# Cross-attention on one core: score tiles from one product over four heads and two products of 154 columns, with second copies of the high queries made by GpSimd

## The chip, the core and the metric

The kernel runs on one core of a Trainium2 chip. A core has five engines with a queue each, which run in order and wait for each other through semaphores: TensorE (PE in the profile; its weight loads are listed apart as PEld), VectorE (DVE), ScalarE (ACT), GpSimd (POOL) and SyncE (SP), which here issues nearly all DMAs. The metric is the device time of one execution in microseconds. A trace of one execution gives the start and the duration of every instruction.

## The reference, cut to what matters

There are 32 sequences of 512 query rows with 640 channels, and 77 key rows of 1024 channels for each sequence. Twenty heads of 32 channels attend; the result goes through an output matrix, and a bias and the input are added. The slices for the object, other and ip branches are empty, since the context has only the 77 text rows, and add nothing.

```python
residual = hidden_states
ehs_txt = encoder_hidden_states[:, :77]
q = _heads(hidden_states @ to_q_w)
s = jnp.einsum('bhqd,bhkd->bhqk', q, _heads(ehs_txt @ to_k_w)) / sqrt(32)
p = jax.nn.softmax(s, axis=-1)
out = _merge(jnp.einsum('bhqk,bhkd->bhqd', p, _heads(ehs_txt @ to_v_w)))
out = out @ to_out_w + to_out_b + residual
```

All of it is in float32. TensorE gets its operands in the type fp32r, which holds fewer bits. The kernel therefore splits a matrix into a high part (a cast on ScalarE) and a low part (the source less the high part, on VectorE or GpSimd) and adds three products: high by high, high by low, low by high. These are the three entries of `PAIRS` (L127).

## The kernel before

**Prologue (to about 274 us).** The context is transposed and split, keys and values of all sequences are computed with the 640 channels on partitions, and both are written to DRAM as high and low parts (`split_keys`, L207, tile `k_dram`, L97; `split_values`, L221). `split_keys` has its high cast, its low subtract and one DMA for each group of 512 key rows and each chunk of channels; groups but the last go through the GpSimd queue, the last through SP.

**Slots.** The channels make 5 chunks of 128, which is four heads each. A slot (`slot(n)`, L660) is one chunk j of one sequence b, n = 5b + j, 160 slots in all. One slot works on many things at once, because stages of earlier chunks are dealt out over later slots:

- `queries(n+1)` (L428): 15 products of 512 columns give the next chunk's queries, transposed (channels on partitions), in one PSUM bank `pq`. `split_q(n+1)` (L442) casts them on ScalarE to `qt[:, 0]` and subtracts on VectorE to `qt[:, 1]`.
- `scores(n, t)` for t = 0 to 3 (L447): for 128 queries the scores against all four heads at once. The keys `kb` are block diagonal (head i has its 32 partitions and its 77 columns, the rest is zero), so 128 channels by 308 columns give 4 heads of 77 scores. Three products of 308 columns make one tile `sc` (3 buffers). Then VectorE takes the negated maximum `nm` of each head (L461).
- `exps(n, t)` (L466): four exponentials on ScalarE for each tile, with row sums.
- `sums` and `normalize(n-1)` (L479, L484): the reciprocals on VectorE and one multiply on GpSimd over the whole chunk of the slot before.
- `transpose_p(n-1)` (L490): a 32 by 32 block transpose on VectorE into the single buffer `z`, then four DMAs to a DRAM tile `pd`. One slot later `load_p` (L506) reads it back as `raw`, with keys on partitions, and again one slot later `cast_p`, `rest_p` and `last_p` (L513 to L533) split it: two casts on ScalarE, one subtract on VectorE and one subtract of 64 partitions on GpSimd.
- `values` (L539): 6 products of 512 columns into `pa`; `sum_a`, `high_a`, `low_a` (L553 to L572) fold and split the result to `at`.
- `piece` (L603): parts of the output projection of the sequence before, 24 products of 320 columns in a slot, into two banks `po`. `finish` (L611) adds residual and bias from `xr` on VectorE, which frees the bank, and stores. `load_residual` (L574) loads `xr`, `add_bias` (L580) adds the bias to it on GpSimd.
- For the next sequences: `load_x`, `transpose_x`, `split_x` (L244 to L264); `refill` (L647) loads the next keys and values.

**What sets the order.** The program is scheduled by hand: the queue of each engine follows the order of the calls in `slot`. In a steady slot GpSimd has `last_p`, `normalize`, then `add_bias` (L706, in all slots but j = 1), then the low parts of `split_x` (two in slot j = 2, three in slot j = 3). VectorE has, in the middle of the slot, the transpose to `z`, the subtract of `split_q`, the maximum of score tile 3, `finish`. ScalarE goes from the exponentials of score tile 3 to `cast_p`, `high_a` and `rest_p` of the next slot. SP issues `load_keys` in slots j = 0 and j = 2 (four DMAs each, two before `load_p` and two behind), `load_values` in slots 1 and 3, `load_x` in slot 4, and `load_residual` in slots 1 to 4. The bias of a residual tile is added one slot after the load: tile 3, loaded in slot 4, in slot 0.

Of the kernel before, what the change touches and what calls it, by code (L numbers as in the profile page):

```python
# [8 lines left out]
F32 = mybir.dt.float32  # L9
FPR = mybir.dt.float32r  # L10
AF = mybir.ActivationFunctionType
ALU = mybir.AluOpType
# [39 lines left out]
def kernel(  # L52
# [49 lines left out]
    def split(hi, lo, src):  # L102
        nc.scalar.copy(hi, src)  # L103
        nc.vector.tensor_tensor(lo, src, hi.bitcast(F32), ALU.subtract)
# [102 lines left out]
    def split_keys(g, j):  # L207
        g0, gn = GROUPS_KV[g]
        ks = kvt.tile([P, 2, G], FPR, tag="ks", name="ks")
        split(ks[:, 0, :gn], ks[:, 1, :gn], pks.pop(j)[:, :gn])  # L210
        engine = nc.gpsimd if g + 1 < len(GROUPS_KV) else nc.sync
        engine.dma_start(
            k_dram[:, j, :, g0 : g0 + gn].bitcast(F32), ks[:, :, :gn].bitcast(F32)
        )

    def values_of(g, j, pool):

# [175 lines left out]
    nc.sync.dma_start(bias, bo.unsqueeze(0).to_broadcast([P, C]))  # L393
    kbs, vbs, pnb = [], [], []
    for g, (j0, nj) in enumerate(GROUPS):
        kb = main.tile([P, nj, 2, KCOLS], FPR, name=f"kb{g}")
        nc.gpsimd.memset(kb.bitcast(F32), 0.0)
        kbs.append(kb)
    for n in range(2):
        pn = main.tile([P, NQ * HPC, KPAD], F32, name=f"pn{n}")  # L400
        nc.gpsimd.memset(pn, 0.0)
        pnb.append(pn)
    qts = [main.tile([P, 2, S], FPR, name=f"qt{n}") for n in range(2)]
    z = main.tile([P, NBLK, NQ, Q], F32, name="z")
    for g, (j0, nj) in enumerate(GROUPS):
        vb = main.tile([P, nj, 2, 2, P], FPR, name=f"vb{g}")
# [2 lines left out]

    def load_keys(b, g, heads=range(HPC)):  # L410
        j0, nj = GROUPS[g]
        src = k_dram[:, j0 : j0 + nj, :, b * NKEY : (b + 1) * NKEY].bitcast(F32)
        for i in heads:
            r = slice(i * HD, (i + 1) * HD)
            nc.sync.dma_start(kbs[g][r, :, :, i * NKEY : (i + 1) * NKEY].bitcast(F32), src[r])

    def load_values(b, g, segments=SEGMENTS):
        j0, nj = GROUPS[g]
# [23 lines left out]
    def split_q(n):  # L442

        qt, pq = qts[n % 2], pqs.pop(n)
        split(qt[:, 0, :], qt[:, 1, :], pq)

    def scores(n, t):  # L447
        b, j = divmod(n, NC_)
        g = GROUP_OF[j]
        qt, kb = qts[n % 2], kbs[g]  # L450
        sc = ps.tile([P, S], F32, tag="sc", name="sc", bufs=3)
        for m, (a, c) in enumerate(PAIRS):
            nc.tensor.matmul(  # L453
                sc[:, :KCOLS],
                qt[:, a, t * P : (t + 1) * P],
                kb[:, j - GROUPS[g][0], c],
                start=(m == 0),
                stop=(m == 2),
            )
        nm = main.tile([P, HPC], F32, tag="nm", name="nm", bufs=3)  # L460
        nc.vector.tensor_reduce(  # L461
            nm, sc[:, :KCOLS].rearrange("p (h k) -> p h k", k=NKEY), AX.X, ALU.max, negate=True
        )
        return sc, nm
# [95 lines left out]
    def high_a(n):  # L560
        if n >= N - NC_ + 1:
            at = xpool[0].tile([P, 2, S], FPR, tag="xt", name="at", bufs=7)
        else:
            at = late[0].tile([P, 2, S], FPR, tag="at", name="at", bufs=8)
        nc.scalar.copy(at[:, 0, :], pas[n][:, 0])
        ats[n] = at
# [93 lines left out]
    def slot(n, beside=()):  # L660
        b, j = divmod(n, NC_)
        ahead, more = n + 1 < N, b + 1 < B
        back, first = PIECES[j]
        bo_, has_out = b - back, b >= back
        xsplits = SPLIT_X.get(j, ((), ())) if more and n > LATE else ((), ())
        turns = TRANSPOSE_X.get(j, ((), (), ())) if more and b else ((), (), ())
        if b == 1 and j < 2:
            turns = (((), (), ()), ((0, 1), (2,), ()))[j]
        taken = takes.get(n)

        filling = taken is not None and not has_out
        if not filling:
            refill(b, j, 0)
        if taken is not None:
            cast_p(taken)
        if n - 1 in takes:
            high_a(takes[n - 1])
        s = scores(n, 0)
        if taken is not None:
            rest_p(taken)  # L680
        rs = sums(n - 1) if n else None
        if taken is not None:
            last_p(taken)
        if n:
            normalize(n - 1, rs)
        if n - 1 in takes:
            low_a(takes[n - 1])
        exps(n, 0, *s)
        if ahead:
            queries(n + 1, 0, 2)  # L690
        s = scores(n, 1)
        if n - LAG + 1 in pds and n > LATE:
            load_p(n - LAG + 1)
        if filling:
            refill(b, j, 0)
        if n == NC_:
            load_x(b + 1, (2, 3))
        for k in WO.get(n, ()):
            nc.sync.dma_start(wos[0][:, k].bitcast(F32), wo_dram[:, k].bitcast(F32))
        refill(b, j, 1)  # L700
        finish()
        if j == 4 and b and b + 2 < B:
            load_x(b + 2, (0, 1))
        if j in RESIDUAL and b >= RESIDUAL[j][0]:
            load_residual(b - RESIDUAL[j][0], RESIDUAL[j][1])
        if j in BIAS and b >= BIAS[j][0]:  # L706
            add_bias(b - BIAS[j][0], BIAS[j][1])
        exps(n, 1, *s)
        for i in turns[0]:
            transpose_x(b + 1, i)  # L710
        if ahead:
            queries(n + 1, 2, NC_)
        s = scores(n, 2)
        if not ahead:
            exps(n, 2, *s)
            piece(bo_, first)
            s = scores(n, 3)
        if j == 3 and has_out:
            piece(bo_, first)
            finish()  # L720
        if n and has_out:
            transpose_p(n - 1)
        if ahead:
            split_q(n + 1)
            exps(n, 2, *s)
        if n and not has_out:
            transpose_p(n - 1)
        if j == 4 and b + 2 < B:
            load_x(b + 2, (0, 1) if not b else (2, 3))
        for c in xsplits[0]:  # L730
            split_x(b + 1, c)
        if not ahead:
            exps(n, 3, *s)
            finish()
            piece(bo_, first + 1)
            take(taken)
            return
        if has_out:
            if j != 3:
                piece(bo_, first)  # L740
        else:
            s = scores(n, 3)
        if taken is not None:
# [158 lines left out]
```

## Time and profile before

| | |
|---|---|
| median of 3 runs | 1960.85 us (1959.88 to 1962.95) |
| profiled execution, its own time | 1961.89 us |
| its span | 1959.8 us |
| granted TensorE clock over the span | 0.992 |
| busy share of PE, PEld, ACT, DVE, POOL | 97%, 87%, 78%, 73%, 51% |
| DMA packets | 568279 (431.28 MB, mean 220 GB/s) |
| score products (L453) | 1920 of 308 columns, 379.1 us busy |
| exponentials (L471) | 2560 of 128x77 |
| normalize (L486) | 160, mean 2278 ns |
| transpose to z (L493) | 160, mean 1512 ns |
| subtract of split_q (L104) | 160 of 128x512, mean 654 ns |
| add_bias (L581) | 128 of 128x640, mean 1576 ns |

The busy share of PE counts overlapping matmuls with modelled ends, so that it says little about how much time a shorter matmul would save. The chain of waits names the work that ended last at each moment; it says more about what sets the end. Times inside a slot are read from the timelines of the engines.

### The profile page before, as it was taken

What the parts mean: (1) busy time and instruction counts of PE and PEld (TensorE: products, weight loads), DVE (VectorE), ACT (ScalarE), POOL (GpSimd) and SP (SyncE); (2) the same over time, 40 slices, a digit from 0 to 9 for tenths busy, and PEclk for the clock granted to TensorE, in tenths of its full rate; (3) what the DMA queues carried; (4) which work ended last, traced back from release to release, by engine and by line L of the source; (5) the groups of instructions that cost most, each with busy time, mean ns of one, the idle gap of its engine ahead of it and who ended that gap; (6) DMA issues with size and microseconds to landing.
All of it is one profiled execution on the core that took longest, in us unless ns stands there. A gap on an engine that the chain in (4) does not pass through costs nothing.

```text
span 1959.8 us, 36241 instructions
## 1 busy us (share of the span) xinstructions
PE 1909.2 (97%) x10332; PEld 1704.8 (87%) x10332; DVE 1436.2 (73%) x2334; ACT 1534.3 (78%) x6210; POOL 1002.3 (51%) x648
## 2 busy tenths in 40 slices
PE   9999997899999999999999999999999999999997
PEld 7787896798988989989999988889989998988896
DVE  4444345778788888888888777787878878878774
ACT  3232237888889888888888888899888988888982
POOL 1000033655566555555556555666556665566643
PEclk9999998999999999999999999999999999999999
DMA  9878869888888888888998888888898888888874
GB/s 187 185 182 234 197 159 238 219 226 226 226 229 234 223 234 232 231 228 222 235 236 230 230 212 238 229 235 223 226 235 231 226 228 226 226 226 228 226 212 135
DMA packets 568279, 431.28 MB, mean 220 GB/s; under 512 B 195344, under 2 KB 477072, under 8 KB 568080
## 3 DMA queue, kind: packets, MB, share of 16 engines
q1 hardware_dynamic: 564848, 417.65, 83.0%
q0 software_dynamic: 3136, 11.14, 1.6%
q8 instruction: 84, 1.38, 0.3%
q14 instruction: 115, 0.94, 0.2%
q10 hardware_dynamic: 96, 0.16, 0.0%
HBM read 247.17 MB, written 181.64 MB: 219 GB/s over the span
## 4 chain that ended last, share of the span: by engine, by line
PE 21%; DMA 19%; issue 17%; ACT 16%; DVE 12%; POOL 11%; SPq 3%; DVEq 0%; POOLq 0%; ACTq 0%
DMA raw<-pd 8%; ACT pn L471 8%; DMA pd<-z 8%; POOL pn L486 7%; PE pq L434 6%; PE po L588 6%; POOL pp L531 3%; DVE pp L524 3%; PE pv L191 3%; PE sc L453 2%; PE pk L191 2%; ACT xt L262 2%; ACT aw L556 2%; DVE nm L461 2%; DVE z L493 2%
## 5 line engine op out<-in xcount | busy, mean ns | idle before, releaser
L471 ACT ACTIVATE pn<-sc,nm 128x77 f32<-128x77 f32 x2560 | 802.6, 335 | 76.6 <-DVE nm L461 74.3
L588 PE MATMUL po<-wo_s,at 128*128 128x320 f32 x3840 | 626.0, 311 | 21.5 <-DVE xr L617 14.2
L434 PE MATMUL pq<-xt,wq_s 128*128 128x512 f32 x2400 | 605.7, 393 | 0.0
L588 PEld LDWEIGHTS po<-wo_s,at 128*128 128x128 f32 x3840 | 576.6, 189 | 32.2 <-DVE xr L617 24.6
L531 POOL TENSOR_TENSOR pp<-raw,pp 64x512 fp32r<-64x512 f32 x160 | 211.1, 1319 | 663.6 <-ACT pp L523 390.4
L471 ACT ACTIVATION_READ_ACCUMULATOR pn<-sc,nm 128x1 f32 x2560 | 545.2, 213 | 0.0
L434 PEld LDWEIGHTS pq<-xt,wq_s 128*128 128x128 f32 x2400 | 437.0, 188 | 75.2
L453 PE MATMUL sc<-kb,qt 128*128 128x308 f32 x1920 | 379.1, 306 | 13.9 <-ACT pn L471 10.4
L486 POOL TENSOR_TENSOR pn<-pn,rs 128x1232 f32<-128x1232 f32 x160 | 364.4, 2278 | 32.9 <-DVE rs L481 20.5
L453 PEld LDWEIGHTS sc<-kb,qt 128*128 128x128 f32 x1920 | 325.5, 189 | 59.3 <-ACT pn L471 12.3
L493 DVE STREAM_TRANSPOSE z<-pn 128x1280 f32<-128x1280 f32 x160 | 241.8, 1512 | 176.1 <-POOL pn L486 166.7
L461 DVE TENSOR_REDUCE nm<-sc 128x4 f32<-128x308 f32 x640 | 294.5, 462 | 41.3 <-PE sc L453 39.2
L524 DVE TENSOR_TENSOR pp<-raw,pp 128x1024 fp32r<-128x1024 f32 x160 | 195.5, 1222 | 91.8 <-ACT pp L517 86.7
L545 PE MATMUL pa<-pp,vb 128*128 128x512 f32 x960 | 253.3, 399 | 1.6 <-DVE pp L524 0.8
L558 DVE TENSOR_TENSOR pa<-pa,aw 64x512 f32<-64x512 f32 x320 | 222.7, 696 | 31.5 <-ACT aw L556 22.2
L263 POOL TENSOR_TENSOR xt<-xs,xt 128x512 fp32r<-128x512 f32 x160 | 204.4, 1296 | 37.8 <-ACT xt L262 36.9
L556 ACT COPY aw<-pa 64x1024 f32<-64x1024 f32 x160 | 162.0, 1013 | 69.5 <-PE pa L545 66.7
L545 PEld LDWEIGHTS pa<-pp,vb 128*128 128x128 f32 x960 | 175.3, 189 | 32.2 <-DVE pp L524 1.1
L517 ACT CAST pp<-raw 128x1024 fp32r<-128x1024 f32 x160 | 168.8, 1055 | 43.2 <-DMA raw<-pd 43.0
L581 POOL TENSOR_TENSOR xr<-xr,bias 128x640 f32<-128x640 f32 x128 | 201.6, 1576 | 0.1
L191 PE MATMUL pk<-ct,wk_s 128*128 128x512 f32 (+1 forms) x600 | 140.5, 394 | 8.2 <-ACT ct L103 6.3
L191 PEld LDWEIGHTS pk<-ct,wk_s 128*128 128x128 f32 x600 | 116.2, 195 | 30.8 <-ACT ct L103 7.2
(42 smaller groups left out, 1347.0 us busy)
## 6 DMA issues: line engine op xcount, KB each, us to landing
pd<-z SPq DMA_DIRECT2D x640, 160.0 KB, 3.9
raw<-pd SPq DMA_DIRECT2D x160, 512.0 KB, 4.0
xs<-in_x_dram SPq DMA_DIRECT2D x128, 320.0 KB, 6.2
xr<-in_x_dram SPq DMA_DIRECT2D x128, 320.0 KB, 4.1
out_dram<-xr SPq DMA_DIRECT2D x127, 320.0 KB, 4.1
raw<-pd SPq DMA_DIRECT2D x160, 128.0 KB, 4.2
v_dram<-vs SPq DMA_DIRECT2D x80, 192.0 KB, 3.9
k_dram<-ks POOLq DMA_DIRECT2D x20, 512.0 KB, 3.4
```

The source lines that it names most:

```text
L191: nc.tensor.matmul(held[j][:, :gn], w[:, k, a, :], cts[g, k][:, c, :gn], start=(k == 0 and n == 0), stop=(k == NK - 1 and n == 2),)
L434: nc.tensor.matmul(pqs[n], wq_s[:, k, a, j * P : (j + 1) * P], xts[b, k][:, c, :], start=(k == 0 and m == 0), stop=(k == NC_ - 1 and m == 2),)
L453: nc.tensor.matmul(sc[:, :KCOLS], qt[:, a, t * P : (t + 1) * P], kb[:, j - GROUPS[g][0], c], start=(m == 0), stop=(m == 2),)
L461: nc.vector.tensor_reduce(nm, sc[:, :KCOLS].rearrange("p (h k) -> p h k", k=NKEY), AX.X, ALU.max, negate=True)
L471: nc.scalar.activation(pnb[n % 2][:, at, :NKEY], sc[:, i * NKEY : (i + 1) * NKEY], AF.Exp, bias=nm[:, i : i + 1], accum_out=sms[n][:, at : ...
L486: nc.gpsimd.tensor_tensor(pf, pf, rs.unsqueeze(2).to_broadcast([P, NQ * HPC, NKEY]), ALU.mult)
L493: nc.vector.transpose(z.rearrange("p b t j -> p t b j"), pn.rearrange("p (t h) k -> p t (h k)", t=NQ).rearrange("p t (b i) -> p t b i", i=Q),)
L524: nc.vector.tensor_tensor(pp[:, 2:4, :], raw[:, 0:2, :], pp[:, 0:2, :].bitcast(F32), ALU.subtract)
L531: nc.gpsimd.tensor_tensor(pp[64:, 4, :], raw[:64, 2, :], pp[:64, 4, :].bitcast(F32), ALU.subtract)
L545: nc.tensor.matmul(pas[n][:, p, :], vb[:, p, t, :], pp[:, c, :], start=(c == p), stop=(t == 1),)
L558: nc.vector.tensor_tensor(pa[64 * p : 64 * p + 64, 0], pa[:64, p], aw[:, p], ALU.add)
L588: nc.tensor.matmul(pos[b, t, h][:, :HALF], ats[b * NC_ + j][:, a, t * P : (t + 1) * P], wos[0][:, j, c, h * HALF : (h + 1) * HALF], start= ...
```

## The change

The high queries by the low keys, and the low queries by the high keys, were two products of 308 columns, each over all four heads. Now one product has 154 columns and serves two heads: its stationary operand `qt[:, 1]` has the low queries of heads 0 and 1 in partitions 0 to 63 and a copy of their high queries in partitions 64 to 127; the keys `kc[..., 0]` have the high keys of heads 0 and 1 in partitions 0 to 63 and their low keys in 64 to 127. The sum over 128 partitions is both cross products at once. `qt[:, 2]` and `kc[..., 1]` do the same for heads 2 and 3. The product of high by high stays as it was, with keys `kb`.

`split_q` now has one cast on ScalarE, two copies of 64x512 on GpSimd that move the high queries to the other half of the partitions, and two subtracts of 64x512 on VectorE in place of one of 128x512. `load_keys` issues two DMAs for each head, one for `kb` and one for `kc`. `split_keys` writes `k_dram` with three DMAs in place of one, in another order of the parts. `add_bias` moves: in slots 0, 2 and 3 it stands ahead of `scores(n, 0)`, and with that ahead of `last_p` and `normalize` in GpSimd's queue; in slot 4 it stands behind the copies.

```diff
-        engine.dma_start(
-            k_dram[:, j, :, g0 : g0 + gn].bitcast(F32), ks[:, :, :gn].bitcast(F32)
-        )
+        dst = k_dram.rearrange("(h r) c w n -> r c w h n", h=2)[:, j, :, :, g0 : g0 + gn]
+        engine.dma_start(dst[:, 0].bitcast(F32), ks[:64, :, :gn].bitcast(F32))
+        for half in range(2):
+            engine.dma_start(dst[:, 1, half].bitcast(F32), ks[64:, 1 - half, :gn].bitcast(F32))
...
-        kb = main.tile([P, nj, 2, KCOLS], FPR, name=f"kb{g}")
+        kb = main.tile([P, nj, KCOLS], FPR, name=f"kb{g}")
+        kc = main.tile([P, nj, 2, KCOLS // 2], FPR, name=f"kc{g}")
...
-    qts = [main.tile([P, 2, S], FPR, name=f"qt{n}") for n in range(2)]
+    qts = [main.tile([P, 3, S], FPR, name=f"qt{n}") for n in range(2)]
...
-            r = slice(i * HD, (i + 1) * HD)
-            nc.sync.dma_start(kbs[g][r, :, :, i * NKEY : (i + 1) * NKEY].bitcast(F32), src[r])
+            r, half = slice(i * HD, (i + 1) * HD), i % 2 * NKEY
+            nc.sync.dma_start(
+                kb[r, :, i * NKEY : (i + 1) * NKEY].bitcast(F32), src[r, :, i // 2, :]
+            )
+            nc.sync.dma_start(kc[r, :, :, half : half + NKEY].bitcast(F32), src[r])
...
-        split(qt[:, 0, :], qt[:, 1, :], pq)
+        nc.scalar.copy(qt[:, 0, :], pq)
+        lower, upper = slice(0, 64), slice(64, P)
+        halves = ((lower, upper), (upper, lower))
+        for w, (r, other) in enumerate(halves):
+            nc.gpsimd.tensor_copy(qt[other, 1 + w, :], qt[r, 0, :].bitcast(F32))
+        for w, (r, other) in enumerate(halves):
+            nc.vector.tensor_tensor(
+                qt[r, 1 + w, :], pq[r], qt[r, 0, :].bitcast(F32), ALU.subtract
+            )
...
-        for m, (a, c) in enumerate(PAIRS):
+        half = KCOLS // 2
+        for m, (cols, keys_) in enumerate(
+            (
+                (slice(0, KCOLS), kb[:, jg]),
+                (slice(0, half), kc[:, jg, 0]),
+                (slice(half, KCOLS), kc[:, jg, 1]),
+            )
+        ):
             nc.tensor.matmul(
-                sc[:, :KCOLS],
-                qt[:, a, t * P : (t + 1) * P],
-                kb[:, j - GROUPS[g][0], c],
+                sc[:, cols],
+                qt[:, m, t * P : (t + 1) * P],
+                keys_,
...
+        bias_now = j in BIAS and b >= BIAS[j][0]
+        if bias_now and (j != 4 or not ahead):
+            add_bias(b - BIAS[j][0], BIAS[j][1])
         s = scores(n, 0)
...
-        if j in BIAS and b >= BIAS[j][0]:
-            add_bias(b - BIAS[j][0], BIAS[j][1])
         exps(n, 1, *s)
...
             split_q(n + 1)
+            if bias_now and j == 4:
+                add_bias(b - BIAS[j][0], BIAS[j][1])
             exps(n, 2, *s)
```

More of the change, by code (lines that the diff above doesn't have):

```diff
@@ L395 @@
     for g, (j0, nj) in enumerate(GROUPS):
-        kb = main.tile([P, nj, 2, KCOLS], FPR, name=f"kb{g}")
-        nc.gpsimd.memset(kb.bitcast(F32), 0.0)
-        kbs.append(kb)
+        kb = main.tile([P, nj, KCOLS], FPR, name=f"kb{g}")
+        kc = main.tile([P, nj, 2, KCOLS // 2], FPR, name=f"kc{g}")
+        for tile_ in (kb, kc):
+            nc.gpsimd.memset(tile_.bitcast(F32), 0.0)
+        kbs.append((kb, kc))
     for n in range(2):
@@ L411, in load_keys @@
         j0, nj = GROUPS[g]
+        kb, kc = kbs[g]
         src = k_dram[:, j0 : j0 + nj, :, b * NKEY : (b + 1) * NKEY].bitcast(F32)
         for i in heads:
-            r = slice(i * HD, (i + 1) * HD)
-            nc.sync.dma_start(kbs[g][r, :, :, i * NKEY : (i + 1) * NKEY].bitcast(F32), src[r])
+            r, half = slice(i * HD, (i + 1) * HD), i % 2 * NKEY
[3 more added lines that the diff above has]
+            nc.sync.dma_start(kc[r, :, :, half : half + NKEY].bitcast(F32), src[r])
     def load_values(b, g, segments=SEGMENTS):
@@ L449, in scores @@
         g = GROUP_OF[j]
-        qt, kb = qts[n % 2], kbs[g]
+        qt, (kb, kc) = qts[n % 2], kbs[g]
+        jg = j - GROUPS[g][0]
         sc = ps.tile([P, S], F32, tag="sc", name="sc", bufs=3)
-        for m, (a, c) in enumerate(PAIRS):
+        half = KCOLS // 2
[6 more added lines that the diff above has]
+        ):
             nc.tensor.matmul(
-                sc[:, :KCOLS],
-                qt[:, a, t * P : (t + 1) * P],
-                kb[:, j - GROUPS[g][0], c],
+                sc[:, cols],
+                qt[:, m, t * P : (t + 1) * P],
+                keys_,
                 start=(m == 0),
```

## The prediction

> **What bounds the kernel now.** I read the busy shares first:
>
> ```profile
> PE 1909.2 (97%) x10332; PEld 1704.8 (87%) x10332; DVE 1436.2 (73%) x2334; ACT 1534.3 (78%) x6210; POOL 1002.3 (51%) x648
> ```
>
> TensorE looks like the bound, and the change takes work from it. The chain of waits, asked for 980 to 1060 us (a steady stretch of eight slots), says otherwise:
>
> ```profile
> 1036.03 1.11 ACT pn L471 x7
> 1037.14 2.06 issue x2
> 1039.20 1.30 POOL pp L531
> 1040.50 0.07 issue
> 1040.57 2.29 POOL pn L486
> 1042.85 0.02 issue
> 1042.88 1.52 DVE z L493
> ...
> 1045.82 5.34 DMA pd<-z
> ...
> 1051.23 6.22 DMA raw<-pd
> ```
>
> Columns: start, length, what held the end. No PE line stands in those 80 us. The chain runs from the exponentials of score tile 3 through ScalarE's casts ("issue x2" covers cast_p, high_a and rest_p), last_p and normalize on GpSimd to the transpose on VectorE. VectorE's timeline shows how it gets back to the exponentials:
>
> ```profile
> 1001.77 1.51 DVE L493 STREAM_TRANSPOSE z<-pn 128x1280 f32<-128x1280 f32 x1 [1.18 <-POOL pn L486]
> 1003.21 0.65 DVE L104 TENSOR_TENSOR qt<-pq,qt 128x512 fp32r<-128x512 f32 x1
> 1003.78 0.46 DVE L461 TENSOR_REDUCE nm<-sc 128x4 f32<-128x308 f32 x1
> ```
>
> The reader is to see that the subtract of split_q lies between the transpose and the maximum of tile 3, which the exponentials of tile 3 wait for (ScalarE: from 1004.37). That closes a loop of one slot. Slot 4 to slot 0, 992.15 to 1001.74 us: transpose 1.55, subtract 0.58 (start to start), maximum 0.46, exponentials 1.23, casts 2.08, last_p 1.41, normalize 2.36 with the small gaps, 9.6 us and no idle link. Over 28 sequences normalize ends follow each other by means of 9.58 (slot 4 to 0), 11.11 (0 to 1), 10.16 (1 to 2), 9.88 (2 to 3) and 10.32 us (3 to 4): 51.05 a sequence. What exceeds 9.58: in 0 to 1, cast_p waits 1.28 us (plus an overlap of 0.12) for raw; in 1 to 2, high_a waits some 0.4 behind VectorE; in 2 to 3 the exponentials come 0.34, in 3 to 4 0.77 us after the maximum, since ScalarE has split_x casts.
>
> ```profile
> DVE z L493 <- POOL pn L486: 166.7, 148, 2.6
> ACT pp L517 <- DMA raw<-pd: 43.0, 31, 3.7
> ```
>
> In this list of waits (total, times, longest) the transpose waits for normalize in 148 of 160 slots, and cast_p for a DMA once per sequence. TensorE's timeline, at the end of slot 0:
>
> ```profile
> 1003.50 1.03 PE L588 MATMUL po<-wo_s,at 128*128 128x320 f32 x6
> 1004.70 1.15 PE L588 MATMUL po<-wo_s,at 128*128 128x320 f32 x6 [0.16 <-DVE xr L617]
> 1005.69 0.59 PE L453 MATMUL sc<-kb,qt 128*128 128x308 f32 x3
> ```
>
> Once a sequence it waits for VectorE and loses 0.66 us on the mean; slots 1 to 4 take 10.08 to 10.11. TensorE alone needs about 50.4 us a sequence, just under the loop's 51.05. Both run nearly full, and the loop is the longer.
>
> **The change part by part.** *Score products.* Starts follow each other by 0.142 us at 308 columns, 0.147 at 320 and 0.230 at 512: a line of 0.43 ns a column plus 9 ns. After the wait above, six products of 320 take 0.99 us (1004.70 to 1005.69) where six take 0.875: a weight load that nothing hides costs 0.115. A product of 154 columns streams in 0.066 us and can't hide that. So it costs 0.076 (the line) to 0.124 (the load and 9 ns); I take 0.124, since the load has a row of its own and the line is only drawn out to 154. A tile goes from 0.426 to 0.390: 20 tiles save 0.7 us a sequence (2.6 at the other end). It is off the loop: nothing gained at the end.
>
> The Trainium skill (TensorE: Matmul & The Clock Gate, section LDWEIGHTS) speaks against halving the columns: a weight load takes its columns over 1.2 GHz whatever the rows, so 107 ns for 128, more than the 66 ns of the stream; the 0.115 agrees. With 107 ns and 9 a tile would save 0.052, 1.0 us a sequence, and with the same page's gap of an isolated matmul, 67 ns, 3.0; the end would be the same by either.
>
> *Two subtracts for one, on the loop.* Rows by form:
>
> ```profile
> L558 DVE TENSOR_TENSOR pa<-pa,aw 64x512 f32<-64x512 f32 x320 | 222.7, 696 | 31.5 <-ACT aw L556 22.2
> L104 DVE TENSOR_TENSOR qt<-pq,qt 128x512 fp32r<-128x512 f32 x160 | 104.7, 654 | 7.8 <-ACT qt L103 7.8
> ```
>
> 64 partitions are no cheaper than 128. The second subtract adds 0.58 us between transpose and maximum in every slot. In 1 to 2 it counts fully, +0.58; in 2 to 3 ScalarE's 0.34 hides part, +0.24; in 3 to 4 the 0.77 hides it. If ScalarE were free there, +0.9 more. Behind the longer VectorE queue wait the maximum, the residual add and TensorE's bank.
>
> *Copies.* No row has a GpSimd copy. Below: memset of 1232 and 1848 elements takes 1127 and 1643 ns, a line that gives 0.53 us at 512. Above: the two-input 64x512 of last_p, 1.32. I take 0.75, since a copy has one input like the memset but reads too. They start when normalize ends, beside the transpose and the subtracts, and end before those or with them; TensorE reads them over 2 us later. At 1.32 each, split_x and bias behind them make last_p 0.35 us late in slot 3, +0.35 a sequence.
>
> The Trainium skill (GPSIMD Engine Reference, section 3.1) measured 769 ns for 512 elements; no run here shows it, and the sum doesn't need it.
>
> *add_bias ahead of last_p.* In slots 2 and 3 GpSimd is idle there (last_p waited 4 to 6 us and 1.4 to 2 us) and xr landed about 2.5 us before last_p. In slot 4 it stands behind the copies, off the loop. Slot 0 is the trouble: SP issues that load late in slot 4, among input loads and stores of z.
>
> ```profile
> 991.27 0.49 SPq L577 DMA_DIRECT2D xr<-in_x_dram  x1
> 996.23 1.60 SPq L251 DMA_DIRECT2D xs<-in_x_dram  x2
> 998.77 0.94 SPq L415 DMA_DIRECT2D kb<-k_dram  x2
> 1000.29 0.38 SPq L509 DMA_DIRECT2D raw<-pd  x1
> ```
>
> Its landings, taken one by one, come 3.9 to 8.4 us after the issue, median 6.8, which is 0.24 us after last_p starts. The loop gives it 0.58 more; bias takes 1.58: last_p and normalize stand 1.3 us behind it (0 if it lands 1.3 us sooner, 2.9 with the latest).
>
> *Key loads.* Slots 0 and 2 get four more DMAs, each about 0.47 us of SP; no more than two stand ahead of raw. In slot 0 the raw load already waits for pd; two more issues cost 0 to 0.94, 58 KB more in front of it 0.25 at 228 GB/s. I take +0.6 of 0 to 1.2. In slot 2 cast_p has over 2 us to spare. If that cover were gone, a second +0.6.
>
> *Slots 4 to 0 to 1 together*, from the transpose of slot 4 to cast_p of slot 1. The engines' side: 2 x 0.58 + 1.3 = 2.46 more, less the 1.40 it waited, +1.06. The DMA side: +0.6. The later one counts, one by one over 27 sequences +1.2 on the mean.
>
> *Prologue.* GpSimd issues 3 DMAs for 1, 20 times, at up to 0.73 us each (the k_dram row): 29 us, beside 239 us of idle GpSimd before 274 us. ScalarE waits 36 us for those landings already, TensorE hardly: +2 us with the first ten slots, 0 to 10.
>
> **Sum:** 0.58 + 0.24 + 1.2 = 2.0 us for each of 29 full sequences, 58; with 2 for the start, +60. Of the profiled execution's 1961.9 that makes 2022; it stands 1 us above the median, so **2021 us**.
>
> **The rivals.** *TensorE sets the pace after all* (not slower). The profile says that it infers releasers; TensorE has no idle in slots 1 to 4, and ScalarE's aw waits for it in slots 0, 1 and 4 (0.7, 0.4, 0.3 us on the mean). If the loop only follows TensorE and has at least 2.0 us of room a sequence that the chain doesn't show, the 0.7 to 2.6 saved on TensorE count: 29 times that is 20 to 75, 1886 to 1941 us, and 1941 by the price taken. Against it: after each aw the exponentials wait once more for the maximum, and the chain has no PE line. Chance 0.12.
>
> *The bias add in slot 0 doesn't wait.* If SP's later queue leaves xr landing 1.3 us earlier, the pair costs the DMA side's 0.6: 1.42 x 29 = 41, 2003 us. For it, landings scatter by 4.5 us; against it, SP's order ahead of that load is unchanged. Chance 0.20.
>
> *Short products are slow.* No row is below 308 columns. If 154 take as long as 512, 0.230, TensorE needs 50.4 + 20 x (0.142 + 0.460 - 0.426) = 53.9 a sequence: +2.9 x 29 = 83, 2045 us, and more beyond. It decides from 0.21 us per product on. Against it, all four sizes lie on one line. Chance 0.10.
>
> **How the numbers follow.** The forecast has 0.55 (its own range 2003 to 2045), the other 0.03 is no change. Low end of the slower cases: no bias wait, no DMA cost, 0.82 x 29 = 24, 1985 us. High end: bias wait 1.55 and DMA 1.2 (pair +1.6), slow copies 0.35, 2.8 x 29 = 80 and 10 for the prologue, 2050. I widen to 1978 to 2056, which leaves out the first rival and half of the third. A change under 0.2% can't be told from none. Slower: 0.55 + 0.20 + 0.10 = 0.85; same 0.03; faster 0.12.
>
> **What would show it.** Right: the chain still without PE; two subtracts of about 0.65 us between transpose and maximum; normalize from slot 4 to 0 over 10.1 us; bias of slot 0 waiting for xr, last_p starting as it ends; new TensorE waits for VectorE or GpSimd in each slot; 154-column starts 0.08 to 0.12 apart. Wrong: subtracts well under 0.58, a loop that has room, or PE lines in the chain.

## The result, and the profile after

The changed kernel takes 2112.44 us (median of 4 runs, 2107.1 to 2117.95); the kernel before took 1961.53 us (1959.88 to 1962.95) in the same comparison. The ratio is 1.077 (95% interval 1.0748 to 1.0792): 151 us slower, 2.5 times the 60 us that the prediction gave. The profiled execution took 2117.95 us, its span is 2116.1 us, and the granted TensorE clock over the span is 0.956 (0.992 before).

The busy line of the page of the changed kernel, and its groups by form (line, engine, operation, tiles, count; busy us, mean ns of one; idle time ahead and what ended it):

```profile
PE 1947.5 (92%) x10332; PEld 1724.5 (81%) x10332; DVE 1583.5 (75%) x2494; ACT 1540.0 (73%) x6210; POOL 1253.5 (59%) x1010
```

```profile
L611 PE MATMUL po<-wo_s,at 128*128 128x320 f32 x3840 | 654.5, 319 | 113.9 <-DVE xr L640 107.7 <-DVE at L593 4.4 <-ACT at L588 1.8
...
L458 DVE TENSOR_TENSOR qt<-pq,qt 64x512 fp32r<-64x512 f32 x320 | 214.5, 670 | 9.8 <-ACT qt L452 5.3
L604 POOL TENSOR_TENSOR xr<-xr,bias 128x640 f32<-128x640 f32 x128 | 207.3, 1621 | 121.7 <-DMA xr<-in_x_dram 95.6 <-PE sc L476 13.1 <-issue 5.2
...
L456 POOL CAST qt<-qt 64x512 fp32r<-64x512 f32 x320 | 195.3, 610 | 40.8 <-ACT qt L452 22.9
```

The subtracts and the copies last what the rows of before let one expect (670 and 610 ns). What grew is a wait in the first line: TensorE waits 107.7 us for VectorE's `finish` (`xr`) to free a `po` bank. The same row before, with 14.2 us:

```profile
L588 PE MATMUL po<-wo_s,at 128*128 128x320 f32 x3840 | 626.0, 311 | 21.5 <-DVE xr L617 14.2 <-DVE at L570 4.4 <-ACT at L565 1.5
```

The place is the end of slot 0, once a sequence. TensorE's timeline there (start, length, instruction, in brackets the idle time ahead and what ended it):

```profile
1017.49 1.08 PE L611 MATMUL po<-wo_s,at 128*128 128x320 f32 x6
1022.66 1.97 PE L611 MATMUL po<-wo_s,at 128*128 128x320 f32 x6 [4.08 <-DVE xr L640]
1024.42 0.46 PE L476 MATMUL sc<-kb,qt 128*128 128x308 f32 x1
1024.68 0.54 PE L476 MATMUL sc<-kc,qt 128*128 128x154 f32 x2
1025.02 2.85 PE L441 MATMUL pq<-xt,wq_s 128*128 128x512 f32 x6
```

Before, the same place showed an idle time of 0.16 us (at most 1.06 us in any steady slot). Now TensorE stands for 4.08 us, and the products that follow are slow: six of 512 columns take 2.85 us (1.58 in slot 0). The stretches of one sequence, a slot each from j = 0 to 4, show why (start and end, length, busy time of the engines, granted clock, DMA share, GB/s):

```profile
1008.89:1024.42 15.53, 11.05 (x59) 9.76 (x58) 11.54 (x19) 10.82 (x46) 8.05 (x6) 0.92 1.03 242
1024.42:1036.33 11.91, 11.91 (x59) 10.63 (x58) 9.06 (x15) 7.43 (x34) 7.04 (x5) 0.81 0.68 180
1036.33:1046.16 9.83, 9.83 (x59) 8.91 (x58) 8.76 (x15) 8.86 (x35) 6.45 (x6) 1.00 0.75 193
1046.16:1055.98 9.82, 9.82 (x59) 8.91 (x58) 8.06 (x14) 9.46 (x39) 8.53 (x7) 1.00 0.88 213
1055.98:1066.02 10.04, 10.03 (x59) 8.96 (x58) 7.73 (x14) 9.20 (x39) 8.18 (x8) 1.00 0.84 207
```

After the stand the granted clock is below 1 in slots 0 and 1. Over the steady slots 10 to 154 the clock is at half speed for 126.3 us, in 29 stretches of one or two pieces of 3.41 us, one stretch a sequence; before it never was. Slots 2 to 4 take 9.8 to 10.0 us, less than the 10.1 of before: the shorter products are in there.

What makes VectorE late is seen on GpSimd and VectorE in the same slot 0:

```profile
1012.52 2.51 POOL L604 TENSOR_TENSOR xr<-xr,bias 128x640 f32<-128x640 f32 x1 [2.87 <-DMA xr<-in_x_dram]
1015.11 1.30 POOL L554 TENSOR_TENSOR pp<-raw,pp 64x512 fp32r<-64x512 f32 x1
1016.48 2.27 POOL L509 TENSOR_TENSOR pn<-pn,rs 128x1232 f32<-128x1232 f32 x1
```

```profile
1012.37 1.23 DVE L547 TENSOR_TENSOR pp<-raw,pp 128x1024 fp32r<-128x1024 f32 x1
...
1018.79 1.51 DVE L516 STREAM_TRANSPOSE z<-pn 128x1280 f32<-128x1280 f32 x1 [3.72 <-POOL pn L509]
1020.22 1.35 DVE L458 TENSOR_TENSOR qt<-pq,qt 64x512 fp32r<-64x512 f32 x2
1021.60 0.48 DVE L484 TENSOR_REDUCE nm<-sc 128x4 f32<-128x308 f32 x1
1022.11 0.49 DVE L640 TENSOR_TENSOR xr<-po,xr 128x320 f32<-128x320 f32 x1
```

The bias addition waits for its load, `last_p` and `normalize` stand behind it, the transpose waits 3.72 us, the two subtracts follow it, and the residual add that frees TensorE's bank is the fourth behind the transpose. The chain of waits, followed from there, now has TensorE in it for the whole of slots 1 and 2 (the lines to the first products of slot 1):

```profile
1020.22 0.64 DVE qt L458
...
1020.88 0.69 DVE qt L458
...
1021.60 0.48 DVE nm L484
...
1022.11 0.50 DVE xr L640
...
1022.66 1.97 PE po L611 x6
1024.63 0.60 PE sc L476 x3
1025.23 2.65 PE pq L441 x6
```

From normalize end to normalize end, means over 28 sequences, in us:

| step | 4 to 0 | 0 to 1 | 1 to 2 | 2 to 3 | 3 to 4 | sequence |
|---|---|---|---|---|---|---|
| before | 9.58 | 11.11 | 10.16 | 9.88 | 10.32 | 51.05 |
| after | 11.49 | 11.34 | 11.92 | 10.44 | 10.42 | 55.61 |
| more | 1.91 | 0.23 | 1.76 | 0.56 | 0.10 | 4.56 |

The 156.3 us between the two spans lie as follows: 8.8 ahead of the first score (274.5 to 283.3), 9.5 in the first ten slots, 131.2 in the next 29 sequences (4.5 each), 6.8 behind.

### The profile page after: what moved, and what is told of

Same layout as the page of the kernel before. It is cut to its first block, busy times and chain, and to the rows that moved or that the text cites. A ratio compares the mean times of both kernels' runs of the same rounds, so it can differ in the third digit from the quotient of the medians.

```text
span 2116.1 us, 37530 instructions
## 1 busy us (share of the span) xinstructions
PE 1947.5 (92%) x10332; PEld 1724.5 (81%) x10332; DVE 1583.5 (75%) x2494; ACT 1540.0 (73%) x6210; POOL 1253.5 (59%) x1010
## 4 chain that ended last, share of the span: by engine, by line
PE 26%; DMA 15%; POOL 14%; DVE 13%; issue 9%; ACT 6%; SPq 3%; DVEq 0%; POOLq 0%; ACTq 0%
PE pq L441 10%; PE po L611 9%; POOL pn L509 8%; POOL pp L554 5%; DMA pd<-z 4%; PE sc L476 4%; DVE qt L458 4%; PE pa L568 3%; DVE z L516 3%; DMA xs<-in_x_dram 3%; ACT pn L494 3%; DMA raw<-pd 3%; DVE nm L484 2%; DVE pa L581 2%; DMA out_dram<-xr 2%
## 5 line engine op out<-in xcount | busy, mean ns | idle before, releaser
L611 PE MATMUL po<-wo_s,at 128*128 128x320 f32 x3840 | 654.5, 319 | 113.9 <-DVE xr L640 107.7
L441 PE MATMUL pq<-xt,wq_s 128*128 128x512 f32 x2400 | 654.3, 415 | 0.0
L441 PEld LDWEIGHTS pq<-xt,wq_s 128*128 128x128 f32 x2400 | 454.8, 201 | 82.1
L554 POOL TENSOR_TENSOR pp<-raw,pp 64x512 fp32r<-64x512 f32 x160 | 237.4, 1484 | 411.9 <-ACT pp L546 301.3
L476 PEld LDWEIGHTS sc<-kc,qt 128*128 128x128 f32 x1280 | 225.5, 198 | 48.2 <-issue 20.2
L476 PE MATMUL sc<-kc,qt 128*128 128x154 f32 x1280 | 244.3, 265 | 16.1 <-POOL xr L604 11.7
L547 DVE TENSOR_TENSOR pp<-raw,pp 128x1024 fp32r<-128x1024 f32 x160 | 213.6, 1335 | 42.6 <-ACT pp L540 42.6
L458 DVE TENSOR_TENSOR qt<-pq,qt 64x512 fp32r<-64x512 f32 x320 | 214.5, 670 | 9.8 <-ACT qt L452 5.3
L456 POOL CAST qt<-qt 64x512 fp32r<-64x512 f32 x320 | 195.3, 610 | 40.8 <-ACT qt L452 22.9
L476 PE MATMUL sc<-kb,qt 128*128 128x308 f32 x640 | 202.5, 316 | 16.7 <-ACT pn L494 11.9
```

The costliest lines, as they stand in the source:

```text
L441: nc.tensor.matmul(pqs[n], wq_s[:, k, a, j * P : (j + 1) * P], xts[b, k][:, c, :], start=(k == 0 and m == 0), stop=(k == NC_ - 1 and m == 2),)
L458: nc.vector.tensor_tensor(qt[r, 1 + w, :], pq[r], qt[r, 0, :].bitcast(F32), ALU.subtract)
L476: nc.tensor.matmul(sc[:, cols], qt[:, m, t * P : (t + 1) * P], keys_, start=(m == 0), stop=(m == 2),)
L547: nc.vector.tensor_tensor(pp[:, 2:4, :], raw[:, 0:2, :], pp[:, 0:2, :].bitcast(F32), ALU.subtract)
L554: nc.gpsimd.tensor_tensor(pp[64:, 4, :], raw[:64, 2, :], pp[:64, 4, :].bitcast(F32), ALU.subtract)
L611: nc.tensor.matmul(pos[b, t, h][:, :HALF], ats[b * NC_ + j][:, a, t * P : (t + 1) * P], wos[0][:, j, c, h * HALF : (h + 1) * HALF], start= ...
```

## The experiments

The theory after the result: the loop of the prediction is right, and what it lacked is that a late slot 0 reaches TensorE through the `po` bank, after which the clock halves. Rivals: GpSimd's new work (copies, bias additions) is what counts; TensorE is the bound after all; the key DMAs cost more than they seemed to. Each ratio below is to the kernel before in the same comparison (medians 1957.2 to 1959.1 us); step times and waits are from the profiled execution.

**The bias additions alone.** The kernel before with only the calls of `add_bias` moved:

```diff
+        bias_now = j in BIAS and b >= BIAS[j][0]
+        if bias_now and (j != 4 or not ahead):
+            add_bias(b - BIAS[j][0], BIAS[j][1])
         s = scores(n, 0)
...
-        if j in BIAS and b >= BIAS[j][0]:
-            add_bias(b - BIAS[j][0], BIAS[j][1])
...
             split_q(n + 1)
+            if bias_now and j == 4:
+                add_bias(b - BIAS[j][0], BIAS[j][1])
```

> The kernel before with only the bias additions at their new places. Theory 1 (the bias addition of slot 0 waits for its residual tile, holds last_p and normalize back, and VectorE then frees the output bank so late that TensorE stands still and its clock falls): a good part of the loss is here already. The wait of slot 0 alone is 0.24 + 1.58, about 1.9 us a sequence, of which cast_p's wait for raw can hide 1.4 on the loop but nothing of it at the bank: 1975 to 2020 us. Theory 2 (the second subtract lengthens the loop in every slot and carries the loss): 1961 us, no change. Theory 3 (the extra key DMAs carry it): 1961 us.

Measured: 2052.98 us, ratio 1.0483 (1.0462 to 1.0504). That is no theory's number: it is above the 2020 of the first, and the other two had no change. The step 4 to 0 grows by 1.60 us, as the waiting load says (1.3 was forecast); but 1 to 2 grows by 1.34 too, where no bias addition holds anything up. TensorE stands 2.1 us a sequence for `xr`, and the clock is at half speed for 75.1 us.

**The second subtract alone.** The kernel before, its one subtract of 128x512 cut into two halves of 64 partitions, with the same result:

```diff
-        split(qt[:, 0, :], qt[:, 1, :], pq)
+        nc.scalar.copy(qt[:, 0, :], pq)
+        for r in (slice(0, 64), slice(64, P)):
+            nc.vector.tensor_tensor(
+                qt[r, 1, :], pq[r], qt[r, 0, :].bitcast(F32), ALU.subtract
+            )
```

> The kernel before with split_q's subtract done as two halves of 64 partitions; the same result. Theory 1: +0.58 in the step from slot 1 to 2, +0.24 from 2 to 3, the rest hidden behind cast_p's wait for raw and ScalarE: 0.82 x 29 = 24 us, 1985 us (1975 to 2000). Theory 2: over 2040 us. Theory 3: 1985 at most.

Measured: 2055.46 us, ratio 1.0502 (1.0486 to 1.0518). Missed by 70 us; theory 2 has the number (over 2040), but not the place, since the loss is no equal one in every slot (+0.83, +0.10, +1.61, +0.52, +0.09 us from the step 4 to 0 on). That is what pointed to the bank: nothing but VectorE has more work here, and yet TensorE stands 2.2 us in each sequence. Slot 1 of four sequences (columns as above):

```profile
992.57:1002.63 10.06, 10.06 (x59) 9.17 (x58) 9.10 (x16) 7.94 (x32) 3.66 (x2) 1.00 0.76 212
1045.97:1056.04 10.07, 10.07 (x59) 9.16 (x58) 9.13 (x16) 7.66 (x33) 3.66 (x2) 1.00 0.73 203
1099.48:1110.96 11.48, 11.48 (x58) 10.30 (x58) 9.62 (x16) 8.10 (x35) 3.75 (x2) 0.87 0.71 196
1153.74:1165.40 11.66, 11.66 (x60) 10.41 (x59) 9.67 (x16) 8.40 (x35) 3.65 (x2) 0.85 0.70 195
```

The same work takes TensorE 10.06 us where the clock holds and 11.5 to 11.7 where it is halved for a part of the slot. A whole sequence, from slot 0 to slot 0, takes 54.43 us with a piece at half clock (22 of 28) and 53.44 us without (6), so that by an estimate from these means some 0.8 of the 3.2 us that a sequence has more are the clock's. With the moved bias additions it is 54.18 (22) and 53.13 us (6).

**The bias additions undone.** The changed kernel with `add_bias` back at its old place in every slot.

> The changed kernel with all bias additions back at their old place behind normalize. Theory 1: the long stall of TensorE at the end of slot 0 goes and the clock stays up; what is left is the second subtract and the key loads, 0.58 + 0.24 + 0.6 us a sequence, 41 us, and 18 us that the trace of the changed kernel shows ahead of slot 10: 2000 to 2025 us. Theories 2 and 3: 2080 us or more.

Measured: 2094.06 us, ratio 1.0712 (1.0672 to 1.0752), against the 2000 to 2025 of theory 1; theories 2 and 3 have the number (2080 or more). Added alone the move costs 94 us, taken away it brings 18 by the medians and 11 by the ratios. TensorE still stands 2.4 us behind the subtracts and the clock is at half speed for 112.6 us. The step 4 to 0 falls by 1.06 us, but 3 to 4 grows by 0.92, where `last_p` now lasts 2.15 us. So the parts don't add: each alone is enough to bring the late bank.

**Only the short products.** The kernel before, the second and third product taken over one half of the columns each:

```diff
+            cols = (slice(0, KCOLS), slice(0, half), slice(half, KCOLS))[m]
...
-                sc[:, :KCOLS],
+                sc[:, cols],
...
-                kb[:, j - GROUPS[g][0], c],
+                kb[:, j - GROUPS[g][0], c, cols],
```

> The kernel before with the second and third score product cut to 154 columns each (the low halves of two heads each are left out, so part of the scores' low order is missing). It has the matmul shapes of the changed kernel and nothing else of it. Loop theory (TensorE is not what sets the pace): 1956 to 1963 us, while TensorE's idle time grows by some 2 us a sequence. Rival (TensorE sets the pace): by the starts in the changed kernel's trace (142, 72 and 110 ns) a tile is 0.10 us shorter, 640 tiles, 64 us: 1897 us.

Measured: 1951.34 us, ratio 0.9964 (0.9952 to 0.9976), a little below the loop theory's range. A slot of TensorE falls from 10.1 to 9.8 us, but a sequence only from 51.05 to 50.70, and TensorE stands up to 1.4 us in slot 0 instead, without loss of clock. That the pace is set elsewhere was right. In its list of TensorE's waits (total, times, longest) the stand is the largest:

```profile
PE po L590 <- DVE xr L619: 37.1, 31, 3.0
```

What TensorE saves it spends waiting for VectorE at the bank: 1.2 us each of 31 times.

**The late bank taken away.** In slot 0 the piece and its `finish` go ahead of `split_q` and the transpose, as they already do in slot 3, so that the residual add no longer stands behind them:

```diff
-        if j == 3 and has_out:
+        if j in (0, 3) and has_out:
             piece(bo_, first)
             finish()
...
-            if j != 3:
+            if j not in (0, 3):
                 piece(bo_, first)
```

In the changed kernel:

> The changed kernel with one reordering: in slot 0 the first piece and its finish stand ahead of split_q and transpose_p, as they do in slot 3, so that VectorE frees the output bank before it waits for normalize. The order on TensorE is the same. Amplifier theory (the loop's lateness of slot 0 reaches TensorE through the bank only; the stall of 3.8 us and the half clock behind it cost more than the loop itself): the stall and the half clock go, and the loop alone sets the pace, 9.58 + 0.83 in three steps, 10.7 to 11 in the two others, with the bias addition still in it: 53.5 us a sequence against 55.6, about 2050 us (2030 to 2070). Rival (the loop alone is the whole loss, TensorE only follows): 2100 us or more.

Measured: 2070.22 us, ratio 1.0579 (1.0563 to 1.0594), at the top of the range. That is 42 us less by the medians and 37 by the ratios; the kernel before was 4.3 us faster in this comparison, so the 37 count. No steady slot has a wait for the bank of over 0.5 us any more. TensorE's longest wait in total is now the one for the subtracts, at the score products:

```profile
PE sc L476 <- DVE qt L458: 80.4, 168, 1.6
```

In six of the sequences the clock still falls behind it, in slot 1, for one piece each (20.5 us for 126.3). It shows no cost here: of 28 sequences the five with a fall in them take 54.0 us, the others 54.1. In the kernel with two subtracts:

> The kernel before with the two half subtracts (2055 us) and the same reordering. Amplifier theory: no stall of 2.5 us, no half clock; the loop's own steps remain, 10.41 in three steps and 10.6 to 10.9 in the two others, 52.7 us a sequence against 54.2: 2010 us (1995 to 2020). Rival: 2040 us or more.

Measured: 2020.77 us, ratio 1.0324 (1.0309 to 1.0340), 35 us less, 1 us above the range. The clock is never at half speed in its steady slots; the wait for the bank (68.4 us in all with the late piece) is all but gone from the list of TensorE's waits, whose first line is now the wait for the subtracts:

```profile
PE sc L457 <- DVE qt L447: 32.8, 60, 2.6
...
PE po L592 <- DVE xr L621: 3.0, 1, 3.0
```

In the kernel before:

> The kernel before with the reordering alone. Loop theory: TensorE's wait for the bank (0.66 us a sequence) goes but the loop of 51.05 stays: 1955 to 1961 us. TensorE theory: 1940 us.

Measured: 1951.78 us, ratio 0.9971 (0.9959 to 0.9983), 3 us below the loop theory's range: the same edit is worth some 6 us where the bank was hardly late. So of the changed kernel's loss some 32 us (37 less 6, before rounding) go through the bank and the clock.

With the bank out of the way the second subtract can be priced by itself, from the last two kernels: 69 us. Their sequences differ by 2.28 us, the steps 4 to 0, 0 to 1, 1 to 2, 2 to 3, 3 to 4 by +0.81, -0.19, +0.95, +0.61 and +0.08.

**Slot 0's bias addition by itself.** The changed kernel with the early piece, and slot 0's `add_bias` alone back at its old place.

> The changed kernel with slot 0's piece early (2070 us before) and with slot 0's bias addition alone back at its old place. Theory: last_p of slot 0 no longer waits 0.71 us nor lasts 1.78, the step from slot 4 to 0 comes down from 11.49 to about 10.4, 1.09 x 29 = 32 us less: about 2038 us. Rival (the room is taken by what is late next, cast_p's wait for raw or the copies behind the bias addition): 2060 to 2070 us.

Measured: 2046.18 us, ratio 1.0443 (1.0427 to 1.0459), 24 us less by the medians, 27 by the ratios. The step 4 to 0 falls from 11.49 to 10.43 as expected; 0.2 us of it come back in the other steps.

**The key writes and loads alone.** The kernel before with the key layout of the change; all three products use the first key tile:

```diff
-                sc[:, :KCOLS],
-                qt[:, a, t * P : (t + 1) * P],
-                kb[:, j - GROUPS[g][0], c],
+                sc[:, :KCOLS],
+                qt[:, a, t * P : (t + 1) * P],
+                kb[:, jg],
```

> The kernel before with only the key writes and key loads of the change (three writes for one in the prologue, two loads for one in slots 0 and 2; products of 308 columns against the first key tile, so the scores of the low keys are left out). Theory: the prologue costs about 9 us up to the first score and some more in the first ten slots, the later slots 0 to 0.6 us a sequence: 1968 to 1990 us. Rival (key DMAs are hidden, and the later start of the changed kernel comes from GpSimd's copies and bias): first score within 2 us of the kernel before, 1957 to 1962 us.

Measured: 1990.48 us, ratio 1.0162 (1.0142 to 1.0182). The first score comes at 284.6 us (10.1 later), 4.1 us more are lost in the first ten slots, and the later sequences take 51.58 us (+0.52; the step 0 to 1, where cast_p waits for raw, 11.72 for 11.11). The list of waits up to 285 us names the prologue's part. In the kernel before:

```profile
ACT ks L103 <- DMA k_dram<-ks: 36.1, 10, 8.9
```

With the three writes for one:

```profile
ACT ks L103 <- DMA k_dram<-ks: 47.5, 12, 9.5
```

ScalarE's casts wait 11.4 us longer for the writes to free their tiles.

Set beside the changed kernel with the early piece, the parts do add up, though the last two are measured with the late one: 3.2% with two subtracts, 1.4% for slot 0's bias addition, 1.6% for the key writes and loads, less 0.4% for the short products, are 5.9%, and the changed kernel with the early piece is at 5.8%. Nothing is left for the copies; no run has them alone.

**A better order of the changed kernel, first try.** Early piece, `add_bias` back everywhere, and `split_q` ahead of the transpose, so that the subtracts run while VectorE waits for normalize.

> The changed kernel with bias additions back at their old place, the same reordering, and split_q(n+1) ahead of transpose_p(n-1), so that both subtracts run while VectorE waits for normalize and leave the loop. Loop theory: loop steps of 9.0 to 9.6 and about 10.3 where ScalarE is full; TensorE at 9.83 a slot becomes the bound, 49.5 us a sequence; with 18 us more ahead of slot 10: 1961 + 18 - 46 = 1933 us (1920 to 1960), better than both kernels. Rival (the subtracts' place does not matter, short products and key loads cost): over 2000 us.

Measured: 2039.23 us, ratio 1.0417 (1.0391 to 1.0443). Missed: the rival has the number (over 2000), not the reason. The subtracts wait for ScalarE's cast to `qt`, which ends too late for two of them: they keep the transpose 0.90 us behind normalize in each slot. And in slot 4, behind three low parts of `split_x`, GpSimd's `last_p` and VectorE's `pp` meet, on GpSimd:

```profile
1024.29 3.79 POOL L264 TENSOR_TENSOR xt<-xs,xt 128x512 fp32r<-128x512 f32 x3
1028.16 2.16 POOL L554 TENSOR_TENSOR pp<-raw,pp 64x512 fp32r<-64x512 f32 x1
```

and on VectorE:

```profile
1026.90 2.26 DVE L547 TENSOR_TENSOR pp<-raw,pp 128x1024 fp32r<-128x1024 f32 x1 [0.83 <-ACT pp L540]
```

Alone they last 1.30 and 1.23 us. VectorE's ends (1029.16) 1.08 after GpSimd's `xt` (1028.08), GpSimd's ends (1030.32) 1.16 after VectorE's, as if each had waited for the other to be done. The Trainium skill (SBUF — State Buffer, section Who interferes with whom) says that a VectorE instruction with two SBUF inputs contends with a GpSimd instruction that reads SBUF. These rows agree, and so does the changed kernel's bias addition of 2.51 us above (1.57 alone), which ended 1.43 after the VectorE `pp` beside it.

**Second try.** One subtract of 128 partitions, a third GpSimd copy in place of the second subtract, the early piece, `split_q` first, and `add_bias` of slots 4 and 0 behind the copies:

```diff
-        for w, (r, other) in enumerate(halves):
-            nc.gpsimd.tensor_copy(qt[other, 1 + w, :], qt[r, 0, :].bitcast(F32))
-        for w, (r, other) in enumerate(halves):
-            nc.vector.tensor_tensor(
-                qt[r, 1 + w, :], pq[r], qt[r, 0, :].bitcast(F32), ALU.subtract
-            )
+        nc.vector.tensor_tensor(qt[:, 1, :], pq, qt[:, 0, :].bitcast(F32), ALU.subtract)
+        nc.gpsimd.tensor_copy(qt[:64, 2, :], qt[64:, 0, :].bitcast(F32))
+        nc.gpsimd.tensor_copy(qt[64:, 2, :], qt[64:, 1, :].bitcast(F32))
+        nc.gpsimd.tensor_copy(qt[64:, 1, :], qt[:64, 0, :].bitcast(F32))
```

> The changed kernel with its products and key layout, but one subtract over 128 partitions again (the low queries of both halves at once), three GpSimd copies of 0.61 us in place of two, split_q ahead of the transpose in the queues, slot 0's piece ahead of both, and the bias additions of slots 4 and 0 behind the copies. Theory (loop plus the late bank): the subtract runs while normalize still runs, so the loop step is about 9.0 to 9.6 us where GpSimd is free, TensorE needs 9.83 a slot, no half-clock windows: about 49.5 to 50.8 a sequence, 1930 to 1975 us with 9 to 18 us of prologue. Rival (GpSimd and VectorE slow each other, or the third copy keeps normalize or last_p waiting): steps of 10.5 to 11.3 in the slots with a bias addition, 2000 us or more.

Measured: 2037.71 us, ratio 1.0391 (1.0371 to 1.0411); the rival was right. The step 4 to 0, where GpSimd has no bias addition ahead, is 8.99 us, but `last_p` waits 1.55 to 1.84 us behind other GpSimd work in slots 2 to 4, and cast_p 1.96 us for raw in slot 1.

**The same order without the change.** The kernel before with the early piece and `split_q` ahead of the transpose:

```diff
         if ahead:
+            split_q(n + 1)
...
-            split_q(n + 1)
             exps(n, 2, *s)
```

> The kernel before with slot 0's piece ahead, as in the earlier run at 1951.8 us, and split_q's one subtract ahead of the transpose in VectorE's queue. Theory (the subtract lies in the loop between transpose and maximum): out of the loop it frees 0.5 to 0.6 us a slot, the loop falls to about 9.0 to 9.5, and TensorE's 10.08 a slot is the bound at about 50.4 a sequence: 1935 to 1950 us. Rival (the subtract then waits for ScalarE's qt copy and keeps the transpose waiting): 1960 us or more.

Measured: 1944.01 us, ratio 0.9921 (0.9906 to 0.9935), the fastest of all: it beats both kernels. Of the 0.8%, 0.3% is the early piece and 0.5% the order. VectorE's queue there, with the subtract in time that was idle, and the maximum behind the transpose, now waiting for TensorE:

```profile
994.67 0.68 DVE L104 TENSOR_TENSOR qt<-pq,qt 128x512 fp32r<-128x512 f32 x1
995.27 1.50 DVE L493 STREAM_TRANSPOSE z<-pn 128x1280 f32<-128x1280 f32 x1
997.36 0.48 DVE L461 TENSOR_REDUCE nm<-sc 128x4 f32<-128x308 f32 x1 [0.59 <-PE sc L453]
```

The slots of TensorE take 10.07 to 10.11 us, the sequence 50.45: here TensorE is the bound, as the prediction's 50.4 for TensorE alone has it.

## Why the prediction was wrong

The direction and the bound were right, the size was not: 151 us for 60, above the range.

- **The loop, and TensorE off it: right.** Halving the columns of two products in three gave 0.4%; one more subtract a slot gave 5%. Of the signs listed as right, the two subtracts stand between transpose and maximum (0.64 and 0.69 us), 4 to 0 takes 11.49 us, and `last_p` starts as the waiting bias addition ends. Two did not come: new waits of TensorE stand in slot 0 alone and not in each slot, and of the starts of 154-column products (0.08 to 0.12 us forecast) one is 0.072.
- **"The chain still without PE": wrong, in slots 1 and 2.** The prediction wrote "behind the longer VectorE queue wait the maximum, the residual add and TensorE's bank", named the wait, and gave it no price. That is the step that failed. TensorE's idle time there went from 0.16 to 4.08 us in the sequence shown, and the clock was halved after it. The step 1 to 2, of which the prediction says "it counts fully, +0.58", measured +1.76, and +0.93 with the bank out of the way. Taking the bank away brought 37 of the 151 us back, 6 of which the same edit also brings without the change.
- **The price of the second subtract: too low.** This is the second step that failed: in the sum it brings 24 us (0.82 x 29), by itself it measured 69. 0.58 us, start to start, was the price of an operation that overlaps its successor. The two take 1.37 us where the one took 0.65, and the maximum starts 0.03 us after them rather than 0.08 before the end: +0.83 a step. With this price the prediction's own formula gives 0.83 in 1 to 2, 0.49 in 2 to 3 (0.34 hidden) and 0.06 in 3 to 4 (0.77 hidden), against +0.95, +0.61 and +0.08 measured by itself. Why the second one doesn't overlap was not tried.
- **Bias in slot 0: right in kind.** 1.3 us forecast; 1.60 where it stands alone, 1.06 beside the second subtract. Of the 2.14 us more in 4 to 0 and 0 to 1 together, 1.2 were forecast. There the wait of 1.40 for raw was to hide part, and it does: it is gone in the changed kernel.
- **Key loads: right in the sequence, wrong in the prologue.** +0.52 a sequence alone, for +0.6. But the prologue with the first ten slots cost 14.2 us with the key DMAs alone, and 18.3 in the changed kernel, where 2 (0 to 10) were taken: ScalarE's wait for the writes, seen as 36 us, was held to have room, and it grew to 47.5 with the key DMAs alone (45.8 in the changed kernel).
- **Copies: cheaper than taken** (0.61 for 0.75 us), and by the sum of the parts above without a share in the loss. **Short products: cheaper too.** A tile of three takes 0.32 to 0.33 us in the chain of slots 1 and 2 (0.390 forecast); the rival of slow short products is refuted.
- **The two other rivals** had no share: less work on TensorE brought 0.4%, and the bias addition does wait.

With the right price of the subtract (0.83 + 0.49 + 0.06), the pair at 2 x 0.83 + 1.06 - 1.40 = 1.32, and 18 for the start, the same sum gives 2.70 x 29 + 18 = 96 us. The early piece in the changed kernel left 113 (its ratio of 1.058), of which the steady sequences hold 88 (3.04 each, for 2.70 by the sum); the 17 us between 96 and 113 are in no term and stay open. The rest, 38 of 151, is the bank and the clock.

## What to carry to other kernels

Where a change lengthens a queue, price every engine that waits behind it, and most of all a TensorE that runs nearly full: a stand of 2 us can be followed by 3.41 us at half clock, here worth some 1.0 us a sequence beside the stand. Price an instruction added in front of a waiting one by its whole duration, not by the start-to-start time of a row whose successor overlaps it. Parts that lean on the same slack don't add up, so that undoing one of them says little; and before a kernel is given less work on an engine, see whether an instruction on the path can go into time that is idle, as the subtract did here for 0.5%.

## What the runs showed of the hardware

**A short stand halves the clock.** Idle times of TensorE at the `po` bank in the steady slots, one a sequence, sorted by whether a piece at half clock followed: of up to 1.61 us none (short products; key loads); with the moved bias additions 22 of 29 (the 22 are of 1.87 to 3.23 us, the other seven of 1.54 to 2.68); with two subtracts, nearly all of 2.2 us, 22 of 29; with the bias additions undone (2.0 to 2.4 us) 27 of 29; of 2.72 to 4.08 us in the changed kernel all 29. But with the early piece stands of 1.4 us at the score products were followed by one too. The length of a stand alone doesn't decide.

What does is in the traces. In each of them all stretches at half clock start on one grid of 3.4133 us, from the first to the last (the start times of the 41 in the changed kernel, prologue and end included, all leave a rest of 1.49 us). Cut along this grid, a stretch each line, TensorE's busy time comes first, the granted clock behind the engines. Three pairs, each a window with a stand and the window behind it, the first two from the kernel with two subtracts, the third from the changed kernel with the early piece:

```profile
989.91:993.32 3.41, 1.72 (x11) 1.68 (x12) 3.28 (x6) 1.92 (x9) 0.00 (x0) 1.00 1.11 268
993.32:996.74 3.42, 3.42 (x18) 2.89 (x17) 3.42 (x8) 3.16 (x14) 1.64 (x2) 1.00 0.46 78
...
1095.72:1099.13 3.41, 1.16 (x8) 0.90 (x7) 3.30 (x7) 1.74 (x10) 0.25 (x1) 1.00 1.07 252
1099.13:1102.54 3.41, 3.41 (x12) 2.92 (x11) 3.38 (x6) 2.95 (x11) 0.77 (x1) 0.50 0.56 128
```

```profile
1488.26:1491.67 3.41, 1.63 (x9) 1.16 (x8) 3.32 (x5) 0.60 (x4) 0.71 (x2) 1.00 1.04 211
1491.67:1495.08 3.41, 3.41 (x11) 2.75 (x10) 3.35 (x7) 3.36 (x14) 0.50 (x1) 0.50 0.87 176
```

In the first pair a stand of 2.16 us lies across the edge of two windows and leaves 1.69 us idle in the one shown; the clock holds. In the second 2.25 us are idle and the clock falls; in the third two stands (1.36 and 0.42 us) in one window make 1.78. Over the steady slots of all 14 traces, with the ends of the products as the profile has them, of the windows at full clock with over 1.85 us idle all 98 are followed by one at half clock, with less than 1.66 us none of some 6050, and between them 8 of 20. So what counts here is the idle time within one window, and the limit lies near half of it (1.71 us). The Trainium skill (TensorE: Matmul & The Clock Gate, Part 1) gives a free-running window of 3413 ns, and the grid agrees with it; it has the clock fall after an idle window of that length, and here about half of one was enough.

**Short products run close to the line down to 154 columns.** Within a tile the second of them starts 72 ns after the first, against 142 ns at 308 columns; the prediction's line of 0.43 ns a column plus 9 ns gives 76 ns. The product behind the second one starts after 110 ns, near the 0.115 us that the prediction has for a weight load that nothing hides; whether it is that was not tested.
